# A graph attention kernel: 31 of 512 steps sum both attention products in one accumulator

## The chip, the core and the metric

The kernel runs on one NeuronCore of a Trainium2 chip. TensorE (PE) multiplies, VectorE (DVE) and ScalarE (ACT) work element by element, GpSimd (POOL) does small sums and issues some transfers, and SyncE (SP) issues most of the others. The metric is the device time of one execution in microseconds (us), shorter being better. The kernel before takes 2055.8 us (median of three runs, 2055.79 to 2056.89).

## The reference, cut to what matters

There are 4096 nodes with 512 features, an adjacency matrix A of zeros and ones, and two layers. The change lies in layer 0, an attention with eight heads of 64 features:

```python
feats = jnp.einsum('nf,hfo->hno', X, W)
s_self = jnp.einsum('hno,ho->hn', feats, a_self)
s_neigh = jnp.einsum('hno,ho->hn', feats, a_neigh)
dense = s_self[:, :, None] + s_neigh[:, None, :]
dense = jnp.where(dense > 0, dense, ALPHA * dense)
dense = dense * A[None, :, :]
attn = jax.nn.softmax(dense, axis=-1)
out = jnp.einsum('hij,hjo->hio', attn, feats) + b[:, None, :]
```

After it come a relu, the sum with the input and a layer norm. Layer 1 is an attention among the 128 nodes of each of 32 graphs, with queries, keys and values from 512 x 512 weights, and again a sum and a layer norm.

A pair without an edge has the score 0, so its weight is exp(0) = 1 and not 0. With s the score of the row node, t that of the column node j, E = exp(leaky(s + t)) and f the features of j with the bias, one row of the output is the sum over j of (A (E - 1) + 1) f, divided by the sum of the same weights.

## The kernel before, in words

**What is multiplied.** The kernel writes E as exp(0.2 s) exp(t) max(p, d), where p = exp(0.8 s) depends on the row alone and d = exp(-0.8 t) on the column alone. It divides the whole row by exp(0.2 s); u = exp(-0.2 s) is the factor of what does not carry E. With g = exp(t) f and S the sum of f over all nodes, the numerator is

- `acc`: the sum over j of A max(p, d) g,
- `accf`: minus the sum over j of A f,
- and at the end `y` = (`accf` + S) u + `acc` (lines 1259 and 1267).

**Tiles.** Pairs of heads make four passes (r = 0 to 3), in each of which the 4096 rows come in four chunks of 1024 (c = 0 to 3), and each chunk has 32 steps (j), one for 128 columns of A. A step has a tile `at` of A, 128 x 1024. Its work:

- DVE, line 1475: for each of the two heads one `q` = max(p_row, d) times `at`, 128 x 1024.
- ACT, line 1485 (DVE, line 1480, for the second head of every fourth step): a `mark` that is 1 where A is 1 and p > d, for the sum of the weights.
- PE, line 1499: `accf`, four products of 512 columns, f being held in two parts (`f_s`).
- PE, line 1521: `acc`, eight products of 32 rows of g (`g_s`) with a half of a `q`, four of which stand beside each other in the array.
- PE, line 1536: `dens`, four products of the marks with six numbers of each column, done after every eighth step.

**Stages and cycles.** A setup (to about 156 us) makes features, exponentials and the tables p and u as rows in DRAM (`pu_d`); `p_row` and `u_row` are read back from there for each chunk, spread over all partitions. The first three passes go in cycles of eight steps, the last in groups of four. In a cycle PE does `accf` for all its steps, then `acc` for all, then `dens`. The first pass also turns A: PE transposes (line 610), ACT casts the result to `at` (line 621), and POOL stores it in `at_d`, from which SP loads the tiles of the later passes (line 628). In the second to last chunk of the last pass the groups have pieces of layer 1 between their products, for the two blocks of 512 rows that the chunk before has finished: transposes (line 1075), `zT` (1095 on PE, 1102 on ACT), scores (1122, then `ns` by DVE at 1131 and exponentials by ACT at 1147), values (1167 on PE, `v_t` by DVE at 1175), output (1181 on PE, 1183 on DVE). `PLANS` says which piece stands in which group. After the last chunk a tail of layer 1 alone follows.

**Who waits for whom.** PE executes its instructions as the program is written. The order on DVE, ACT, POOL and SP is made at build time by a planner that goes by priority and by its own costs; each engine then follows its order strictly. `q` has a ring of eight buffers in the first three passes, of six in the last, two being used in each step, so that DVE can be four or three steps ahead of `acc`. `at` has rings of 12 and 6.

**Buffers.** `a4` (line 1080, two of them) holds the diagonal blocks of A for layer 1, `ns` and `pT` (one each) the scores and their transposes. `hst` (one) holds the finished 1024 x 128 tile of a pass. `ck` (two) holds pieces of A that are tested in the passes two to four (line 1222).

Of the kernel before, what the change touches and what calls it, by code (L numbers as in the profile page):

```python
# [404 lines left out]
def adjacency_streamed_path(  # L405
# [55 lines left out]

    g_d = dram.tile([PR, NT // 4, P, 4 * FP], F32, name="g_d")
    f_d = dram.tile([PR, NT // 4, P, 4 * 2 * FP], F32, name="f_d")
    pu_d = dram.tile([2 * H, N], F32, name="pu_d")
    at_d = dram.tile([NCH, NT, P, C], F32, name="at_d")
    hs_d = dram.tile([N, FP * (PR - 1)], F32, name="hs_d")

# [25 lines left out]
    p_all, u_all = pu_all[:, :, 0, :], pu_all[:, :, 1, :]  # L493
    n0 = const.tile([P, NT], F32, name="n0")
    nb_all = const.tile([P, NT, H], F32, name="nb_all")
    e_all = early.tile([P, NT, 2, H], F32, name="e_all")
    e_b = const.tile([P, NT, H, 6], BF16, name="e_b")

# [36 lines left out]
    urowp = ctx.enter_context(tc.tile_pool(name="urows", bufs=1))  # L535
    evp = ctx.enter_context(tc.tile_pool(name="ev", bufs=1))
    hp_ = ctx.enter_context(tc.tile_pool(name="hout", bufs=1))
    ckp = ctx.enter_context(tc.tile_pool(name="ck", bufs=2))
    ps0 = ctx.enter_context(tc.tile_pool(name="ps_misc", bufs=1, space=PSUM))
    banks = [ps0]  # L540

# [90 lines left out]
    with tc.tile_pool(name="setup1", bufs=1, side="right") as one, tc.tile_pool(  # L632
# [97 lines left out]
        def exponentials(k, u, sc):  # L730

            j = 4 * k + u
            if u == 0:
                pu_js[k] = two.tile([P, 4, 2, H], F32, name="pu_j")
            st = small.tile([P, 5, H], F32, name="st")
            for lo, hi, w in ((0, 3, 1), (3, 5, 0)):
                ends_of_setup["DVE", u] = nc.vector.tensor_tensor(
                    st[:, lo:hi].rearrange("p k (q h) -> p k q h", q=2),
                    sc[:, None, :, :, w].to_broadcast([P, hi - lo, 2, H // 2]),
                    powers[:, lo:hi].rearrange("p k (q h) -> p k q h", q=2),  # L740
                    OP.mult,
                )
            nc.scalar.activation(e_all[:, j], st[:, 0:2], AF.Exp)
            nc.scalar.activation(pu_js[k][:, u], st[:, 3:5], AF.Exp)
            nc.scalar.activation(d_all[:, j, :], st[:, 2], AF.Exp)

        def parts_of_exponentials(k):
            blk = slice(4 * k, 4 * k + 4)
            nc.vector.tensor_scalar_mul(
                nb_all[:, blk, :], d_all[:, blk, :], -BIG * (1.0 + 2.0**-23)  # L750
            )
            eb = e_b[:, blk]
            for i in range(2):
                src = e_all[:, blk, i, :]
                rest = small.tile([P, 4, H], F32, name="rest")
                nc.vector.tensor_copy(eb[:, :, :, 3 * i], src)
                nc.vector.tensor_sub(rest, src, eb[:, :, :, 3 * i])
                nc.vector.tensor_copy(eb[:, :, :, 3 * i + 1], rest)
                nc.vector.tensor_sub(eb[:, :, :, 3 * i + 2], rest, eb[:, :, :, 3 * i + 1])
            nc.vector.tensor_copy(  # L760
                e_p[:, blk, :NE].rearrange("p j (m h) -> p j h m", h=H), eb[:, :, :, :3]
            )
            nc.vector.tensor_scalar_mul(eb[:, :, :, :3], eb[:, :, :, :3], -1.0)

        def rows_of_exponentials(k):
            pr = pss.tile([2 * H, 4, P], F32, name="ps_set")
            for u in range(4):
                nc.tensor.transpose(
                    pr[:, u, :], pu_js[k][:, u].rearrange("p k h -> p (k h)"), ident
                )  # L770
            if k < NB - 1:
                row = late.tile([2 * H, 4 * P], F32, name="pu_row")
            else:
                row = hp_.tile([P, CT, FP], F32, name="hst")
                row = row.rearrange("p t n -> p (t n)")[: 2 * H, : 4 * P]
            rows[k] = row
            ends_of_setup["ROW"] = nc.scalar.copy(
                row.rearrange("p (q n k) -> p q k n", q=2, k=2),
                pr.rearrange("p (q k) n -> p q k n", q=2),
            )  # L780
            nc.gpsimd.dma_start(pu_d[:, ts(k, 4 * P)], row)

        def columns_of_exponentials(k, pc=None):
            pc = pss.tile([P, 4, 2 * H], F32, name="ps_set") if pc is None else pc
            for u in range(4):
                nc.tensor.transpose(pc[:, u, :], rows[k][:, ts(u, P)], ident[: 2 * H, : 2 * H])
            nc.vector.tensor_copy(
                pu_all[:, 4 * k : 4 * k + 4].rearrange("p u k h -> p u (k h)"), pc
            )
# [138 lines left out]
    def columns_of_last():  # L928

        columns_of_exponentials(NB - 1, misc([P, 4, 2 * H]))  # L930

    psa = ctx.enter_context(tc.tile_pool(name="ps_acc_f", bufs=1, space=PSUM))
    dens = psa.tile([P, HB], F32, name="dens")
    nc.vector.memset(dens, 0.0)
# [134 lines left out]
    def layer_1(blk, x1b, lp, lp1, lp2):  # L1069
# [45 lines left out]
            if c % 2:  # L1115
                yield
        pq = misc([P, 4, P])
        ns = lp1.tile([P, 4, P], F32, name="ns")
        nm = small.tile([P, 4], F32, name="nm_f")
        for u in range(4):  # L1120
            for f in range(FC):
# [72 lines left out]
        pp = misc([P, 4, P])  # L1194
        for u in range(4):
            nc.tensor.transpose(pp[:, u, :], ns[:, u, :], ident)
        pT = lp1.tile([P, 4, P], F32, name="pT_f")
        nc.scalar.copy(pT, pp)
        values(1)
        yield  # L1200
# [49 lines left out]
    def sums_to_rows(r, c, acc, accf, ae, u_row, later_by):  # L1250
# [25 lines left out]
        def pieces():  # L1276
# [55 lines left out]
            nc.vector.reciprocal(rd, rd)  # L1332
            if r == 0:
                yield later_by
            hst = hp_.tile([P, CT, FP], F32, name="hst")
            for t4 in range(0, CT, 4):
                fin = misc([P, 4, FP])
                for t in range(4):
# [65 lines left out]
    def main_pass(r, ae=None, wide=4):  # L1404

        for c in range(NCH):
# [8 lines left out]
            for h in range(2):  # L1415
                in_order(
                    r == 0 and c < 2,
                    nc.sync.dma_start(
                        u_row[h * FH : (h + 1) * FH, :],
                        broadcast_rows(pu_d[H + 2 * r + h, ts(c, C)], FH, C),  # L1420
                    ),
                )
            def pieces(c, group, place):
                if r == PR - 1 and c:
                    run_plan(PLANS[c == NCH - 1][group][place])
                elif place == (r == 0):
                    run_pieces((0.75 if r else 1.0) * wide)
# [18 lines left out]
            for j0 in range(0, NT, wide):  # L1446
# [13 lines left out]
                    in_order(r == 0 and c == 0 and j0 < 16, ins)  # L1460
                if at_step == 0:
                    cast_steps(0, 6, last_pair)
                follow = [
                    x
                    for x in steps[at_step + wide : at_step + 2 * wide]
# [3 lines left out]
                for j in cycle:  # L1469
                    for h in range(2):  # L1470
                        hh = 2 * r + h
                        q = qs[j, h] = ring("q", qp, 6).tile([P, C], F32, name="q")
                        d_j = d_all[:, j, hh : hh + 1]
                        with following(at_step == 0, ("DVE", 3 if j else 2)):
                            ends_of_setup["Q"] = nc.vector.scalar_tensor_tensor(  # L1475
                                q, p_row[h], d_j, ats[r, c, j].bitcast(F32), op0=OP.max, op1=OP.mult
                            )
                        mark = marks[j, h] = sgp.tile([P, C], FP8, name="mark")
                        if j % 4 == 3 and h == 1:
                            nc.vector.tensor_scalar(  # L1480
                                mark, q, d_j, None, op0=OP.is_gt, saturate=False
                            )
                        else:
                            with following(at_step == 0, "ACT", "ROW"):
                                nc.scalar.activation(  # L1485
                                    mark,
                                    q,
                                    AF.Sigmoid,
                                    bias=nb_all[:, j, hh : hh + 1],
                                    scale=BIG,  # L1490
                                    saturate=False,
                                )
# [1 line left out]
                    with following(True, "Q"):  # L1494
                        parts_of_exponentials(NT // 4 - 1)
                for j in cycle:
                    for w in range(2):
                        for s in range(2):
                            nc.tensor.matmul(  # L1499
                                accf[:, s, :],  # L1500
                                f_s[j // 4][:, j % 4, w, :],
                                ats[r, c, j][:, ts(s, HB)],
                                start=(j == 0 and w == 0),
                                stop=(j == NT - 1 and w == 1),
                            )
# [9 lines left out]
                    pieces(c, j0 // 4, 0)  # L1515

                for j in cycle:
                    for s in range(2):
                        for o in range(0, FP, 32):
                            h = o // FH  # L1520
                            nc.tensor.matmul(  # L1521
                                acc[o : o + 32, s, :],
                                g_s[j // 4][:, j % 4, h, o % FH : o % FH + 32],
                                qs[j, h][:, ts(s, HB)],
                                start=(j == 0),
                                stop=(j == NT - 1),
                            )
                if r == 0:
                    pieces(c, j0 // 4, 1)
# [117 lines left out]
```

## Time and profile before

| | |
|---|---|
| timed runs | 2055.79, 2055.8, 2056.89 us |
| the profiled execution | 2057.91 us, of which 2056.1 us lie between its first and its last instruction |
| PE busy | 2030.4 us (99%) |
| DVE busy | 1671.9 us (81%) |
| ACT busy | 1542.2 us (75%) |
| POOL busy | 224.2 us (11%) |
| granted TensorE clock | 0.994 of full speed |

One execution is recorded; an instruction has a line of the kernel, a start and a length. "Idle before" is the time for which an engine stood still in front of an instruction, and the releaser is what ended it. The chain that ended last is followed back from the last instruction: at each step to what released it, or to the instruction before it on its engine. Instructions of one engine overlap a little at their ends, so that the distance between two starts, and not the length, is what one costs in a dense row.

### The profile page before, as it was taken

Reading aid. Unit: us, or ns where it says so; the run is one execution under the profiler, and the core shown is the slowest. Engines: PE = TensorE matmul, PEld = TensorE weight load, DVE = VectorE, ACT = ScalarE, POOL = GpSimd, SP = SyncE. Lnnn points to the kernel's source line nnn. Section 1 sums busy time; section 2 is a strip of 40 time slices with the busy share of each in tenths; the row PEclk is TensorE's granted clock in tenths of the full one; section 3 lists DMA queues with packets and bytes.
Section 4 is the critical chain, followed back from the end, with each engine's and each line's share of the span. In section 5 each row is a group of like instructions: output and inputs, shape, how many; then the busy total and the mean of one; then the engine's idle time right before and its main releaser. Section 6 shows DMA issues by size and latency. Waiting matters only on the chain.

```text
span 2056.1 us, 38302 instructions
## 1 busy us (share of the span) xinstructions
PE 2030.4 (99%) x15105; PEld 1051.0 (51%) x15105; DVE 1671.9 (81%) x2125; ACT 1542.2 (75%) x1878; POOL 224.2 (11%) x361
## 2 busy tenths in 40 slices
PE   9999999999999999999999999999999999999997
PEld 7884555555544444444454444544454445545453
DVE  5668888888899998798998999999975984896654
ACT  3349888888879889788898989998885666567420
POOL 1222222222100000000000000000210210210111
PEclk9999999999999999999999999999999999999999
DMA  6999999999999999798999999989974764775211
GB/s 208 245 325 259 287 288 276 291 268 289 271 373 337 354 352 335 257 310 298 319 323 340 316 336 323 326 295 358 323 237 144 250 242 137 225 274 169 73 49 43
DMA packets 207371, 551.31 MB, mean 268 GB/s; under 512 B 24780, under 2 KB 65740, under 8 KB 207180
## 3 DMA queue, kind: packets, MB, share of 16 engines
q1 hardware_dynamic: 142828, 426.31, 59.6%
q0 software_dynamic: 62272, 121.91, 23.2%
q8 instruction: 121, 1.98, 0.4%
q10 hardware_dynamic: 2080, 0.52, 0.1%
q14 instruction: 70, 0.57, 0.1%
HBM read 491.79 MB, written 107.22 MB: 291 GB/s over the span
## 4 chain that ended last, share of the span: by engine, by line
PE 93%; DVE 4%; issue 1%; DMA 1%; SPq 0%; POOL 0%; ACT 0%; POOLq 0%; DVEq 0%
PE acc L1521 41%; PE accf L1499 23%; PE ps_fe L800 5%; PE ps_m L1167 5%; PE dens L1536 5%; PE ps_m L1095 5%; DVE q L1475 3%; PE ps_m L1122 1%; PE ps_m L610 1%; PE ps_m L1181 1%; PE ps_m L1075 1%; PE ps_m L1024 1%; PE ps_m L1339 1%; PE ps_set L720 1%; PE ae L1435 1%
## 5 line engine op out<-in xcount | busy, mean ns | idle before, releaser
L1475 DVE SCALAR_TENSOR_TENSOR q<-p_row,d_all,at 128x1024 f32<-128x1024 f32 x1024 | 1242.0, 1277 | 146.9 <-PE acc L1521 121.1
L1485 ACT ACTIVATE mark<-q,nb_all 128x1024 fp8e4<-128x1024 f32 x896 | 995.5, 1145 | 184.3 <-DVE q L1475 168.6
L1521 PE MATMUL acc<-q,g_s 128*32 128x512 f32 x8192 | 903.4, 593 | 1.1 <-DVE q L1475 0.4
L1521 PEld LDWEIGHTS acc<-q,g_s 128*32 128x32 f32 x8192 | 264.1, 110 | 594.4 <-issue 533.0
L1499 PE MATMUL accf<-at,f_s 128*128 128x512 f32 x2048 | 495.2, 398 | 2.1 <-ACT at L621 2.1
L1499 PEld LDWEIGHTS accf<-at,f_s 128*128 128x128 f32 x2048 | 380.3, 188 | 110.4 <-issue 26.4
L1230 ACT ACTIVATE ck<-ck,neg_half_f 128x1024 f32<-128x1024 f32 x128 | 146.0, 1141 | 25.5 <-DMA ck<-in_adj_dram 25.4
L1231 ACT ACTIVATE ck<-ck,neg_quarter 128x1024 f32<-128x1024 f32 x128 | 146.3, 1143 | 1.7
L1536 PE MATMUL dens<-mark,e_b 128*6 128x512 fp8e4 x2048 | 125.3, 379 | 0.0
L800 PE MATMUL ps_fe<-w_sb_f,xT_f 128*128 128x264 f32 (+1 forms) x512 | 121.1, 393 | 1.9 <-ACT xT_f L723 1.9
L621 ACT CAST at<-ps_m 128x1024 fp32r<-128x1024 fp8e4 x124 | 116.4, 1025 | 4.8 <-PE ps_m L610 4.3
L1167 PE MATMUL ps_m<-wvT,x1T 128*128 128x512 f32 x256 | 114.2, 594 | 0.0
L1095 PE MATMUL ps_m<-x1T,M_sb 128*128 128x512 f32 x256 | 112.9, 594 | 0.0
L800 PEld LDWEIGHTS ps_fe<-w_sb_f,xT_f 128*128 128x128 f32 x512 | 100.1, 199 | 16.4 <-ACT xT_f L723 2.5
L1350 POOL DMA_DIRECT2D hs_d<-hst x12 | 10.7, 896 | 847.8 <-DVE hst L1340 847.8
L1480 DVE TENSOR_SCALAR mark<-q,d_all 128x1024 fp8e4<-128x1024 f32 x128 | 96.3, 752 | 4.7
L622 POOL DMA_DIRECT2D at_d<-at x128 | 69.0, 541 | 272.3 <-ACT at L621 248.1
L1536 PEld LDWEIGHTS <-e_b 128*6 128x6 bf16 x2048 | 54.7, 86 | 77.7 <-issue 34.6
L1095 PEld LDWEIGHTS ps_m<-x1T,M_sb 128*128 128x128 f32 x256 | 48.0, 190 | 59.3 <-issue 58.4
L1167 PEld LDWEIGHTS ps_m<-wvT,x1T 128*128 128x128 f32 x256 | 47.6, 190 | 56.4 <-issue 55.2
L1175 DVE TENSOR_TENSOR v_t<-ps_m,bv_row 128x512 f32<-128x512 f32 x32 | 21.7, 684 | 60.5 <-PE ps_m L1167 60.5
L1102 ACT ACTIVATE zT<-ps_m,zb 128x512 f32<-128x512 f32 x32 | 21.7, 680 | 61.2 <-PE ps_m L1095 61.2
(195 smaller groups left out, 1099.5 us busy)
## 6 DMA issues: line engine op xcount, KB each, us to landing
at<-at_d SPq DMA_DIRECT2D x384, 512.0 KB, 6.3
f_s<-f_d SPq DMA_DIRECT2D x128, 512.0 KB, 7.8
at_d<-at POOLq DMA_DIRECT2D x128, 512.0 KB, 14.8
ck<-in_adj_dram SPq DMA_DIRECT2D x128, 512.0 KB, 5.5
g_s<-g_d SPq DMA_DIRECT2D x128, 256.0 KB, 5.6
f_d<-fst POOLq DMA_DIRECT2D x16, 1024.0 KB, 7.9
a_b<-in_adj_dram POOLq DMA_DIRECT2D x32, 512.0 KB, 17.4
p_row<-pu_d SPq DMA_DIRECT2D x32, 512.0 KB, 6.9
```

Of the source, the lines that this page charges most:

```text
L621: ends_of_setup["ACT"] = nc.scalar.copy(at, both[:, :, k])
L800: nc.tensor.matmul(pf[:, q, :, cols], tile_j(xTs[k][:, c].rearrange("p u n -> p (u n)"), u), w_sb[:, c, 4 * q : 4 * q + 4, cols], start=(c ...
L1095: nc.tensor.matmul(pz, L1["M"][:, f, ts(c, P)], x1T[:, f, :], start=(f == 0), stop=(f == FC - 1),)
L1167: nc.tensor.matmul(pv, x1T[:, f, ts(u, P)], L1["wvT"][:, f, :], start=(f == 0), stop=(f == FC - 1),)
L1230: tc.keep_in_program_order(nc.scalar.activation(ck, ck, AF.Square, bias=neg_half))
L1231: nc.scalar.activation(ck, ck, AF.Abs, bias=neg_quarter, accum_out=binp[:, k : k + 1])
L1475: ends_of_setup["Q"] = nc.vector.scalar_tensor_tensor(q, p_row[h], d_j, ats[r, c, j].bitcast(F32), op0=OP.max, op1=OP.mult)
L1480: nc.vector.tensor_scalar(mark, q, d_j, None, op0=OP.is_gt, saturate=False)
L1485: nc.scalar.activation(mark, q, AF.Sigmoid, bias=nb_all[:, j, hh : hh + 1], scale=BIG, saturate=False,)
L1499: nc.tensor.matmul(accf[:, s, :], f_s[j // 4][:, j % 4, w, :], ats[r, c, j][:, ts(s, HB)], start=(j == 0 and w == 0), stop=(j == NT - 1 an ...
L1521: nc.tensor.matmul(acc[o : o + 32, s, :], g_s[j // 4][:, j % 4, h, o % FH : o % FH + 32], qs[j, h][:, ts(s, HB)], start=(j == 0), stop=(j ...
L1536: nc.tensor.matmul(dens[lo : lo + 6, :], e_b[:, j, 2 * r + h, :], marks[j, h][:, ts(s, HB)], start=(j == 0), stop=(j == NT - 1),)
```

## The change

In a folded step `q` is made by two DVE instructions for each head instead of one. With U = 1/u in a new row and 1/exp(t) in a new column, q = (max(p, d) U - 1/exp(t)) A, and q times g is A (E - 1) f. That is the edge's whole share of the numerator, and it belongs to `accf`, which is multiplied by u at the end. So the eight products of line 1521 go into `accf`, and the four of line 1499 are left out. The mark is taken from the sign of q. What the step reads and stores otherwise is as before; `f_s` is loaded for all steps.

Folded are, in the first pass, steps 10 and 18 of the first chunk and 2, 10 and 18 of the others (11), and in the last pass, of the second chunk, one step of group five, two of group six and three of group seven (steps 17; 20, 21; 24 to 26), and of the third and fourth chunk these and step 9 in group three (20 in all).

```diff
+    FOLDED = (0, PR - 1)
+    FOLDS = {4: (1,), 5: (0, 1), 6: (0, 1, 2)}, {2: (1,), 4: (1,), 5: (0, 1), 6: (0, 1, 2)}
+    HU = 2 * len(FOLDED)
...
+            for r in FOLDED:
+                nc.vector.reciprocal(
+                    c_all[r][:, blk], e_all[:, blk, 1, 2 * r : 2 * r + 2]
+                )
...
         def rows_of_exponentials(k):
-            pr = pss.tile([2 * H, 4, P], F32, name="ps_set")
+            for i, r in enumerate(FOLDED):
+                nc.vector.reciprocal(
+                    pu_js[k][:, :, 2 * H + 2 * i : 2 * H + 2 * i + 2],
+                    pu_js[k][:, :, H + 2 * r : H + 2 * r + 2],
+                )
+            pr = pss.tile([2 * H + HU, 4, P], F32, name="ps_set")
...
-        ns = lp1.tile([P, 4, P], F32, name="ns")
+        ns = a4
...
-        pT = lp1.tile([P, 4, P], F32, name="pT_f")
+        pT = a4
...
+            if r == PR - 1:
+                hst = y.rearrange("p (t n) -> p t n", t=CT)
+            else:
+                hst = hp_.tile([P, CT, FP], F32, name="hst")
...
+            def folded(j):
+
+                if r == PR - 1:
+                    return r in FOLDED and c > 0 and j % 4 in FOLDS[c > 1].get(j // 4, ())
+                return r in FOLDED and j % 8 == 2 and (0 if c else 8) < j < NT - 8
+
+            def rows_for_folded():
+
+                for h in range(2):
...
+                    nc.sync.dma_start(
+                        U_row[h],
+                        broadcast_rows(pu_d[2 * H + 2 * FOLDED.index(r) + h, ts(c, C)], P, C),
+                    )
...
+                if any(map(folded, range(NT))) and j0 == (4 if r else 0):
+                    rows_for_folded()
...
+                        if folded(j):
+                            cn = c_all[r][:, j, h : h + 1]
+                            nc.vector.scalar_tensor_tensor(
+                                q, p_row[h], d_j, U_row[h], op0=OP.max, op1=OP.mult
+                            )
+                            nc.vector.scalar_tensor_tensor(
+                                q, q, cn, ats[r, c, j].bitcast(F32), op0=OP.subtract, op1=OP.mult
+                            )
+                            mark = marks[j, h] = sgp.tile([P, C], FP8, name="mark")
+                            nc.scalar.activation(
+                                mark, q, AF.Sigmoid, bias=below_0, scale=2.0**80, saturate=False
+                            )
+                            continue
...
-                    for w in range(2):
+                    for w in range(0 if folded(j) else 2):
...
+                    dst = accf if folded(j) else acc
...
-                                acc[o : o + 32, s, :],
+                                dst[o : o + 32, s, :],
```

The rows U are loaded by SP, two transfers of 512 KB for each chunk that has folded steps: in the first pass into the two buffers of `ck`, which that pass does not use otherwise, and in the last pass into the buffer of `hst` and a new one. For these `ns` and `pT` are given up: they are now written over `a4`, which is therefore held until `pT` has been read. The last pass writes its finished tile over `y`. The pool of `ck` is made after the setup instead of before it.

## The prediction

> **What bounds the kernel now.** I read the page's first two parts and its chain of waits, then the stretches of the four passes, then PE and DVE in order of time in the groups that are to be folded.
>
> ```profile
> PE 2030.4 (99%) x15105; PEld 1051.0 (51%) x15105; DVE 1671.9 (81%) x2125; ACT 1542.2 (75%) x1878; POOL 224.2 (11%) x361
> DVE  5668888888899998798998999999975984896654
> PE 93%; DVE 4%; issue 1%; DMA 1%; SPq 0%; POOL 0%; ACT 0%; POOLq 0%; DVEq 0%
> PE acc L1521 41%; PE accf L1499 23%; PE ps_fe L800 5%; PE ps_m L1167 5%; PE dens L1536 5%; PE ps_m L1095 5%; DVE q L1475 3%; PE ps_m L1122 1%; PE ps_m L610 1%; PE ps_m L1181 1%; PE ps_m L1075 1%; PE ps_m L1024 1%; PE ps_m L1339 1%; PE ps_set L720 1%; PE ae L1435 1%
> L1475 DVE SCALAR_TENSOR_TENSOR q<-p_row,d_all,at 128x1024 f32<-128x1024 f32 x1024 | 1242.0, 1277 | 146.9 <-PE acc L1521 121.1
> ```
>
> PE is the chain from end to end, and 23% of the chain is `accf`, which the change cuts. DVE's main row waits 121.1 us for PE (for a free `q`), so it is ahead of PE. Whether it stays ahead is a question for each stage (window, then busy time of PE, PEld, DVE, ACT, POOL, clock, DMA share, GB/s): a chunk of the first pass, and one of the last.
>
> ```profile
> 266.00:372.00 106.00, 105.66 (x977) 53.49 (x976) 88.08 (x92) 92.48 (x91) 25.75 (x41) 1.00 1.11 280
> 1605.00:1775.00 170.00, 169.65 (x1028) 83.42 (x1028) 127.55 (x197) 109.55 (x148) 22.28 (x37) 1.00 0.63 215
> ```
>
> PE is full in both; DVE has some 18 us of 106 free in the first, 42 of 170 in the second.
>
> In order of time, the first cycle of a chunk of the first pass, PE then DVE:
>
> ```profile
> 371.06 7.60 PE L1499 MATMUL accf<-at,f_s 128*128 128x512 f32 x32
> 378.50 1.07 PE L610 MATMUL ps_m<-ident_b,a_b 128*128 128x128 bf16 x16
> 379.49 13.94 PE L1521 MATMUL acc<-q,g_s 128*32 128x512 f32 x128
> ...
> 370.67 6.06 DVE L1475 SCALAR_TENSOR_TENSOR q<-p_row,d_all,at 128x1024 f32<-128x1024 f32 x5
> 376.83 0.90 DVE L1480 TENSOR_SCALAR mark<-q,d_all 128x1024 fp8e4<-128x1024 f32 x1
> 381.52 10.85 DVE L1475 SCALAR_TENSOR_TENSOR q<-p_row,d_all,at 128x1024 f32<-128x1024 f32 x9 [3.80 <-PE acc L1521]
> ```
>
> DVE fills its eight buffers, stands for 3.80 us, and goes on when the first step of `acc` frees two. In the last pass (DVE, then PE, third chunk, group six):
>
> ```profile
> 1694.06 3.68 DVE L1475 SCALAR_TENSOR_TENSOR q<-p_row,d_all,at 128x1024 f32<-128x1024 f32 x3 [3.68 <-issue]
> 1698.32 6.06 DVE L1475 SCALAR_TENSOR_TENSOR q<-p_row,d_all,at 128x1024 f32<-128x1024 f32 x5
> 1708.29 0.29 DVE L1131 CUSTOM_DVE_ANT_0 ns<-ps_m,a 128x128 f32<-128x128 f32 x1 [3.91 <-PE ps_m L1122]
> ...
> 1699.90 3.91 PE L1499 MATMUL accf<-at,f_s 128*128 128x512 f32 x16
> 1708.18 7.07 PE L1521 MATMUL acc<-q,g_s 128*32 128x512 f32 x64
> ```
>
> **What the Trainium skill says.** "VectorE: DVE Perf Modes", section "The perf-mode tier table", gives two-tensor fp32 instructions one element per cycle and no faster mode. The trace agrees: 128x1024 takes 1277 ns, and nine stand in 10.85 us, a pitch of (10.85 - 1.28) / 8 = 1.197 us. Its section "The DRAIN you can't avoid" says that an instruction starts only when the pipe of the one before is empty. Here that holds for dependent ones alone: line 512 after 1183, whose result it reads, starts 0.78 us behind a start of 0.75 us length, while independent q's overlap by 0.08. So the second of a folded pair costs 1.2 us when the planner puts something between and about 1.3 if not. "TensorE: Matmul & The Clock Gate", "Part 3: Packing small matmuls", lets products in different column groups run at once; 128 of line 1521 in 13.87 us are 0.434 us for each four, and a change of the target bank alters nothing in that. "DMA: Bandwidth & Descriptors", "Issuing engines are not separate DMA queues": all transfers share the 16 engines. In the first pass these show a share of 1.11, so the added 1 MB per chunk, beside 280 GB/s x 106 us = 30 MB, is not free of risk.
>
> **The change part by part.** *Removed on PE:* four `accf` products a step. In the first pass 32 take 378.50 - 371.06 = 7.44 us from start to start, 0.93 a step; in the last 16 take 1664.26 - 1660.53 = 3.73 (group four of that chunk), also 0.93. 31 x 0.93 = 28.8 us. The products into `accf` cost what they cost in `acc`.
>
> *Added on DVE:* two instructions a step, 2 x 1.2 to 1.3 = 2.4 to 2.6 us; ACT makes as many marks as before.
>
> *First pass (11 steps).* The folded step is the third of its cycle, so it falls into the filling of the buffers, where DVE then stands 3.80 (above), 4.86 and 5.19 us. Of 3.80, 2.4 to 2.6 go to the added pair and 0.93 to PE's earlier `acc`: 0.3 to 0.5 are left. Behind that lies another half: step eight of `acc` is due at 379.49 + 7 x 1.734 = 391.6, and its q's end at 391.1. I take no loss. If that cover were gone, each us is paid in full.
>
> *Last pass, group five:* DVE has 3.7 to 7.6 us free (3.68 in the fence), 2.4 to 2.6 are used. Nothing is lost.
>
> *Group six (two folds, 4.8 to 5.2 us):* DVE has eight q's to make from 1694.06 on and ends at 1704.3; folded, at 1709.1 to 1709.5. PE needs 9.13 us from the end of `acc` at 1699.05 to the next, now 7.27: 1706.3. Steps one to three are ready in time, the third by 0.5. Then line 1131 holds DVE for 0.95, and the fourth step's q's (2.4) end at 1712.5 to 1712.9, due at 1706.3 + 3 x 1.75 = 1711.6. PE waits 0.9 to 1.3, unless the planner puts the q's first: I take 0.95, three times, 2.85 us. Late next are `ns` and its exponentials, by about 1.5 us; they are used by line 1196 some 20 us later.
>
> *Group seven (three folds, 7.2 to 7.8 us):* DVE stands 10.41 us in front of `v_t` in the second and third chunk and 9.88 in the fourth. Hidden.
>
> *Group three (one fold, third and fourth chunk):* DVE's six q's end at 1647.24 and both `v_t` follow; folded, the q's end at 1649.7 and `v_t` at 1650.4, while PE wants it for line 1181 at 1650.86 - 0.93 = 1649.9. PE waits about 0.55, twice: 1.1 us.
>
> *Setup:* 32 tiny reciprocals, 0.6 us of each 17 us block in which DVE is busy for two thirds; hidden but for the last block. There the ROW copy of line 777 starts at 156.23 right behind a cast that ended then, and the two reciprocals (0.18 us for four elements, line 1160) stand before its transposes: I take 0.5 us on the chain to the first `accf`.
>
> *SP and buffers:* 14 transfers U_row. In the first pass they come when step 18 of the chunk before frees `ck`, 40 us ahead of use; for the first chunk behind the bias row of 167.24, used at about 187, with 7 us to land. In the last pass they come a chunk ahead. Behind them in SP's queue stand `f_s`, `g_s` and `at` loads; `f_s` is issued near 402 and used at 424.6, so some us of standing are covered. Holding `a4` until `pT` is read moves the loads of line 1080 (1538.79, 1595.45 and so on) to about 1596, 1652 and, for the last block, from 1947 to 1967, where the next loads behind it (1969.09) are not issued earlier anyway. Writing over `y` needs only what was transposed. These cost nothing; the cover is the queue's own waiting.
>
> Sum: 28.8 - 2.85 - 1.1 - 0.5 = 24.35 us. The profiled span goes from 2056.1 to 2031.8; its run took 2057.91, and the median of the runs, 2055.8, goes to **2031.5**.
>
> **The rivals.** *All hidden:* the planner puts `v_t` and the q's that PE waits for first. Then 28.3, 2027.5. For it: each stall above is under 1.3 us. Against: it plans by its own costs, and already now PE waits for q's (2.4 us at 1467, 1.4 at 1614).
>
> *The first pass gives nothing:* the margin of 0.3 us is eaten, by a late U_row, by the loaded DMA engines, or because ACT's marks come later and its casts (line 621) behind them keep PE's transposes waiting. Then 28.8 - 10.2 - 4.45 = 14.1: 2041.7. Against it: 4.86 and 5.19 us in the other cycles, and ACT's 13 us of 106 free.
>
> *The last pass gives its saving back:* DVE's order there is perturbed and the stalls are 18.6 instead of 3.95 us. Only the first pass counts, 9.7: 2046.
>
> *Slower:* in the last pass the longer q's come to stand in front of rows that PE waits for (1131, 1175, 520). Place: groups three and five to seven. The price is the added DVE time that shows, of 20 x 2.6 = 52 us; from 55% of it on (28.3 us) the kernel loses. At 65%: 2061. Against it: DVE's 10.41 us in front of `v_t`, which hold the largest part.
>
> *The change doesn't do what it says:* all folded steps leave `accf`'s products out in the written order of PE, so this rival is only a term of the above.
>
> **How the numbers follow.** The forecast has 0.50 (2028.5 to 2034.5), all hidden 0.18, the first pass giving nothing 0.13, the last giving its saving back, wholly or in part, 0.12, slower 0.06; 0.01 is left for no change. A measurement tells about 0.2% (4 us) from none, and all cases but the last two are beyond it: faster 0.93, same 0.01, slower 0.06. The range runs from 2027 (all hidden) to 2042 (first pass giving nothing, and half of the last pass's case).
>
> **What would show it.** Line 1499 should have 2048 - 124 = 1924 products and 29 us less; line 1521 the same 8192. DVE should be busy some 75 us longer and its idle time before q should fall by about as much as it is covered. In the first pass a chunk should take 103.4 instead of 106.2 us, with DVE still standing before the first q of `acc`, a few tenths in the first cycle. In groups three and six PE should wait 0.5 to 1.3 us for `v_t` and q. I am wrong if PE shows gaps of over 1 us in group five or seven, if U_row ends waits of DVE, or if the tail after the last `dens` (1933.5 to the end) becomes longer than its 122.6 us.

## The result and the profile after

The changed kernel takes 2042.7 us (median of six runs, 2038.29 to 2044.16), the kernel before 2055.8 us (six runs, 2053.32 to 2057.68): a ratio of 0.993, 95% interval 0.992 to 0.995. It is faster by 13 us, where 24 were forecast. The profiled execution took 2043.19 us, its span 2041.3 us, 14.8 us less than before.

The page's busy times, DVE in slices and the chain of waits, of the changed kernel:

```profile
PE 2005.9 (98%) x14981; PEld 1030.0 (50%) x14981; DVE 1744.8 (85%) x2219; ACT 1533.1 (75%) x1872; POOL 231.0 (11%) x362
...
DVE  5668898898999998798999989999997897889754
...
PE 85%; DMA 7%; DVE 5%; issue 1%; ACT 1%; SPq 0%; POOL 0%; POOLq 0%; DVEq 0%; ACTq 0%
...
L1534 DVE SCALAR_TENSOR_TENSOR q<-p_row,d_all,at 128x1024 f32<-128x1024 f32 x962 | 1168.1, 1279 | 106.0 <-PE acc L1581 78.8
...
L1558 PE MATMUL accf<-at,f_s 128*128 128x512 f32 x1924 | 469.3, 400 | 1.7 <-ACT at L628 1.6
```

DVE has 73 us more to do and still waits 78.8 us for PE. `accf` has its 1924 products. New are the transfers, 7% of the chain instead of 1%. Where they stand is told by PE's waits from 150 to 600 us (waited for, us in all, times, longest); the first row and the third are new:

```profile
PE ps_m L617 <- DMA a_b<-in_adj_dram: 6.2, 3, 3.6
PE accf L1558 <- ACT at L628: 1.6, 1, 1.6
PE ps_set L786 <- DVE pu_j L780: 1.2, 1, 1.2
PE ps_m L617 <- DVE hst L1312: 1.1, 3, 0.4
```

PE waits for the pieces of A that are to be turned (`a_b`, loaded by POOL at line 605), once in the first cycle of each chunk but the first. The worst of the three, in order of time on PE, where the prediction showed 371.06 to 379.49 of the kernel before:

```profile
369.24 7.01 PE L1558 MATMUL accf<-at,f_s 128*128 128x512 f32 x28
379.89 1.07 PE L617 MATMUL ps_m<-ident_b,a_b 128*128 128x128 bf16 x16 [3.63 <-DMA a_b<-in_adj_dram]
380.88 5.31 PE L1581 MATMUL acc<-q,g_s 128*32 128x512 f32 x32
386.02 1.89 PE L1581 MATMUL accf<-q,g_s 128*32 128x512 f32 x16
```

The saving is in the first line, 28 products in place of 32. Behind it PE stands for 3.63 us, and the next 32 products take 5.31 us, where the same 32 in the fourth chunk take 3.64.

The stretches, each from the first `accf` product of one pass to that of the next (us):

| | before | after | forecast gain | gain |
|---|---|---|---|---|
| setup, to the first product | 157.8 | 160.2 | -0.5 | -2.4 |
| first pass | 424.0 | 422.8 | 10.2 | 1.2 |
| second and third pass | 772.3 | 772.5 | 0 | -0.2 |
| last pass and tail | 702.0 | 685.8 | 14.65 | 16.2 |
| span | 2056.1 | 2041.3 | 24.35 | 14.8 |

So the last pass gave somewhat more than forecast, the setup lost 2 us more, and nine of the first pass's ten microseconds are missing. By chunk the first pass took 107.1, 106.2, 106.3 and 104.4 us before and takes 104.7, 104.4, 109.3 and 104.4 now: the third chunk loses 3 us, where each should gain 2 to 3.

### The profile page after: what moved, and what is told of

The parts are those of the page before. It is cut to its first block, busy times and chain, and to the rows that moved or that the text cites. A ratio compares the mean times of both kernels' runs of the same rounds, so it can differ in the third digit from the quotient of the medians.

```text
span 2041.3 us, 38200 instructions
## 1 busy us (share of the span) xinstructions
PE 2005.9 (98%) x14981; PEld 1030.0 (50%) x14981; DVE 1744.8 (85%) x2219; ACT 1533.1 (75%) x1872; POOL 231.0 (11%) x362
## 4 chain that ended last, share of the span: by engine, by line
PE 85%; DMA 7%; DVE 5%; issue 1%; ACT 1%; SPq 0%; POOL 0%; POOLq 0%; DVEq 0%; ACTq 0%
PE acc L1581 35%; PE accf L1558 20%; PE ps_fe L818 5%; PE ps_m L1186 5%; PE ps_m L1114 5%; PE dens L1597 5%; DMA a_b<-in_adj_dram 4%; DVE q L1534 3%; PE accf L1581 2%; PE ps_m L1141 1%; PE ps_m L1200 1%; DMA hp_l<-hs_d 1%; PE ps_m L617 1%; DMA at_d<-at 1%; PE ps_m L1043 1%
## 5 line engine op out<-in xcount | busy, mean ns | idle before, releaser
L1534 DVE SCALAR_TENSOR_TENSOR q<-p_row,d_all,at 128x1024 f32<-128x1024 f32 x962 | 1168.1, 1279 | 106.0 <-PE acc L1581 78.8
L1544 ACT ACTIVATE mark<-q,nb_all 128x1024 fp8e4<-128x1024 f32 x834 | 926.8, 1144 | 174.7 <-DVE q L1534 160.1
L1581 PE MATMUL acc<-q,g_s 128*32 128x512 f32 x7696 | 853.7, 594 | 1.1 <-DVE q L1534 0.4
L1581 PEld LDWEIGHTS acc<-q,g_s 128*32 128x32 f32 x7696 | 250.2, 110 | 557.2 <-issue 496.3
L1558 PE MATMUL accf<-at,f_s 128*128 128x512 f32 x1924 | 469.3, 400 | 1.7 <-ACT at L628 1.6
L1558 PEld LDWEIGHTS accf<-at,f_s 128*128 128x128 f32 x1924 | 357.2, 189 | 107.3 <-issue 27.8
L818 PEld LDWEIGHTS ps_fe<-w_sb_f,xT_f 128*128 128x128 f32 x512 | 100.5, 200 | 16.2 <-ACT xT_f L730 2.3
L1529 ACT ACTIVATE mark<-q,below 128x1024 fp8e4<-128x1024 f32 x62 | 69.6, 1153 | 24.5 <-DVE q L1525 24.2
L1525 DVE SCALAR_TENSOR_TENSOR q<-q,c_all,at 128x1024 f32<-128x1024 f32 x62 | 77.3, 1273 | 0.0
```

The source lines that it names most:

```text
L818: nc.tensor.matmul(pf[:, q, :, cols], tile_j(xTs[k][:, c].rearrange("p u n -> p (u n)"), u), w_sb[:, c, 4 * q : 4 * q + 4, cols], start=(c ...
L1534: ends_of_setup["Q"] = nc.vector.scalar_tensor_tensor(q, p_row[h], d_j, ats[r, c, j].bitcast(F32), op0=OP.max, op1=OP.mult)
L1544: nc.scalar.activation(mark, q, AF.Sigmoid, bias=nb_all[:, j, hh : hh + 1], scale=BIG, saturate=False,)
L1558: nc.tensor.matmul(accf[:, s, :], f_s[j // 4][:, j % 4, w, :], ats[r, c, j][:, ts(s, HB)], start=(j == 0 and w == 0), stop=(j == NT - 1 an ...
L1581: nc.tensor.matmul(dst[o : o + 32, s, :], g_s[j // 4][:, j % 4, h, o % FH : o % FH + 32], qs[j, h][:, ts(s, HB)], start=(j == 0), stop=(j ...
```

## Experiments

Each time is the median of its runs, with the lowest and the highest; the ratio is that to the kernel before, run beside it, with its 95% interval. Stretches and waits are those of the one profiled execution.

Three explanations for the missing nine. D1: the transfers were full before, and whatever PE saves it waits. D2: the 1 MB of U rows that the change adds to each chunk makes `a_b` late. D3: the folded steps' marks, which come later on ScalarE, delay the casts behind them, the stores that POOL issues, and so the `a_b` loads in POOL's queue.

### Only the last pass folded, and three cuts in the first pass

The base of the next kernels:

```diff
-    FOLDED = (0, PR - 1)
+    FOLDED = (PR - 1,)
```

> Only the 20 steps of the last pass are folded; the first pass, its reciprocals and its U rows are as before. All theories: the first pass of the changed kernel gained only 0.5 us, the last pass and the tail 16.3 us, so this kernel takes what the changed one takes, 2042 us (2040 to 2044). If instead the first pass's folded steps were worth their 10.2 us in the time and the loss is elsewhere, 2052 us.

2042.49 us (2041.87 to 2045.47), ratio 0.9945 (0.9929 to 0.9962). The 11 folded steps of the first pass are worth nothing. This kernel is the yardstick for the first pass: 423.0 us, no wait for `a_b`.

The changed kernel with the U rows of the first chunk used in all four:

```diff
+                if r == 0 and c:
+                    U_row.extend(rows_of_chunk_0)
+                    return
```

> The changed kernel with the U rows of the first pass loaded for its first chunk only and used again in the other three (which leaves out what those chunks should be multiplied with). DMA engines full already before (D1): 3 MB less of some 160 MB, so at most 3 us of gain and the waits for the tiles a_b stay: 2041 to 2043. The 1 MB of each chunk is what delays the a_b loads (D2): the waits for a_b vanish, 2034 us (2032 to 2036). Folded marks on ScalarE delay the casts, the stores and so the loads (D3): nothing changes, 2042.7.

2033.92 us (2033.15 to 2036.29), ratio 0.9898 (0.9881 to 0.9914). No wait for `a_b` is left and the first pass takes 414.7 us. That is what D2 said, and D1 is out.

The base with PE's part alone, the four `accf` products of the 11 steps left out:

```diff
-                    for w in range(0 if folded(j) else 2):
+                    for w in range(0 if folded(j) or left_out(j) else 2):
```

> As the kernel with the last pass folded alone, and in the first pass the four accf products of the same 11 steps are left out (their share of minus the sum of A f is missing from the result); VectorE, ScalarE and all transfers are as before. TensorE has 10.2 us less work and nothing else changes. D1, DMA full: PE waits for a_b instead, the same time as the last pass alone within 2 us, 2041 to 2043. D2 and D3: the whole 10.2 us appear, 2032 us (2031 to 2034).

2034.53 us (2032.83 to 2035.51), ratio 0.9899 (0.9883 to 0.9916); first pass 415.1 us, 8.0 less than the base. The transfers had room for a shorter PE. Both this run and the one before reach 8.0 to 8.4 of 10 us; in the first cycle of a chunk some 0.6 of the 0.9 is kept, and why was not looked into.

The changed kernel with every second f tile of the first pass not loaded:

```diff
+                    if r == 0 and k % 2 and (c or k > 3):
+                        f_s[k] = f_s[k - 1]
```

> The changed kernel with every second tile of f in the first pass not loaded (its steps use the tile before, so the result of the first pass is wrong): 2 MB of transfers less in each chunk, all else the same. D1 and D2, transfers set the pace: the a_b waits shrink or vanish, 2034 us (2032 to 2038). D3, ScalarE's order sets it: nothing changes, 2041.5 to 2043.5.

2029.81 us (2027.47 to 2030.22), ratio 0.9876 (0.9859 to 0.9892), faster than its range. Other bytes than the U rows serve as well: no wait for `a_b`, first pass 414.0 us. The rest of its lead over the kernel with the rows loaded once lies outside the first pass: its profiled setup ended at 157.5 instead of 160.6, with a granted clock of 1.00 between 20 and 45 us, where that one and the changed kernel show 0.86, and its last pass took 684.0 instead of 686.7 us. Whether the edit has a part in that is open.

### The rows without the shorter PE

If the rows alone make `a_b` late, they must do so while PE has all its work. Two attempts failed. The first loads the rows and uses them nowhere:

```diff
-                return r in FOLDED and j % 8 == 2 and (0 if c else 8) < j < NT - 8
+                return False
...
-                if any(map(folded, range(NT))) and j0 == (4 if r else 0):
+                if (r == 0 or any(map(folded, range(NT)))) and j0 == (4 if r else 0):
```

> The kernel with the last pass folded alone, to which the U rows of the first pass are loaded as in the changed kernel, but nothing reads them. C, a budget: with the rows, the transfers of a chunk need some 105.5 us (the changed kernel's chunk), which still fits into the 105.8 to 106.3 us that TensorE needs when no step is folded: no wait for a_b, the time of the kernel without the rows, 2042.5 us (2041 to 2044). B, a burst: 1 MB issued at once makes the next a_b loads late at any pace: waits for a_b of some us in chunks two to four, 2046 to 2050 us.

2057.52 us (2054.01 to 2060.15), ratio 1.0010 (1.0001 to 1.0019), which nobody expected. With no reader to wait for, SP issued the rows of all four chunks between 169.9 and 193.9 us; PE's waits for the whole execution begin with

```profile
PE accf L1558 <- DMA f_s<-f_d: 12.2, 1, 12.2
```

that is, the f tile of the second cycle stood behind the rows in SP's queue. Chunks two to four, now without any rows to load, took 106.2, 106.3 and 104.4 us as in the base. The second attempt gives the rows a reader, a copy of two numbers where the folded steps would be:

```diff
+                        if touched(j):
+                            nc.vector.tensor_copy(small.tile([P, 2], F32, name="nm_f"), U_row[h][:, :2])
```

> As the kernel with U rows that nothing reads, but two numbers of each row are read by VectorE where the folded steps of the changed kernel would be, so that the rows of a chunk are loaded when those of the chunk before have been used, as in the changed kernel. C, a budget: with the rows the transfers of a chunk need some 105.5 us, less than the 105.8 to 106.3 us of an unfolded chunk on TensorE: 2042.5 us (2041 to 2044), no wait for a_b beyond 1 us. B, a burst makes the loads behind it late at any pace: a_b waits of 2 us or more in a chunk, 2047 to 2050 us.

2065.09 us (2063.59 to 2065.82), ratio 1.0051 (1.0034 to 1.0067). The planner put all these copies, which depend on nothing but the rows, into the first chunk, and DVE waited there six times, 32.7 us in all, for transfers that came behind others. Both kernels say nothing on the question, but they show what a misplaced megabyte costs.

The third keeps everything of the change except PE's saving:

```diff
-                    for w in range(0 if folded(j) else 2):
+                    for w in range(0 if folded(j) and r else 2):
...
-                    dst = accf if folded(j) else acc
+                    dst = accf if folded(j) and r else acc
```

> The changed kernel with VectorE's, ScalarE's and the transfers' part of the first-pass folding left as it is, but TensorE does the four accf products of the 11 steps all the same and sums their q into acc (so A f is counted in excess there). C, a budget: 105.5 us of transfers fit behind 105.8 to 106.3 us of TensorE, no wait for a_b: the time of the kernel with the last pass folded alone, 2042.5 us (2041 to 2044), and TensorE waits only where its work is shortened and the rows are loaded as well. B, the rows as such, or the folded marks on ScalarE, make the a_b loads late: the 6.2 us of a_b waits stay on top of the full work, 2048 to 2051 us.

2042.17 us (2040.45 to 2043.48), ratio 0.9934 (0.9918 to 0.9951): the base's time, first pass 423.1 us, no wait for `a_b`, though the rows were loaded chunk by chunk (from 170.6, 216.7, 321.4 and 427.7 us). B is out: the rows and the folded steps' work on DVE and ScalarE, without the shorter PE, cost nothing. But it was close. PE, and POOL's issue of the load in question, in the third chunk of this kernel:

```profile
373.55 7.60 PE L1558 MATMUL accf<-at,f_s 128*128 128x512 f32 x32
380.99 1.07 PE L617 MATMUL ps_m<-ident_b,a_b 128*128 128x128 bf16 x16
...
353.29 0.90 POOL L605 DMA_DIRECT2D a_b<-in_adj_dram  x1 [0.64 <-DMA at_d<-at]
354.29 0.55 POOL L629 DMA_DIRECT2D at_d<-at  x1
362.52 0.53 POOL L629 DMA_DIRECT2D at_d<-at  x1 [7.69 <-DMA a_b<-in_adj_dram]
```

The load landed 27.6 us after its issue, at 380.9; PE turned its tile at 380.99. The last line shows the other half of the mechanism: POOL issues in order, and a store that has to wait for an earlier load holds up what stands behind it. The same load in five kernels (issue and landing from POOL's transfers, the time PE turns the tile, or would without waiting, from PE in order of time):

| third chunk | issued | us to landing | landed | PE wants it | margin |
|---|---|---|---|---|---|
| before | 350.2 | 13.9 | 364.1 | 378.5 | 14.4 |
| short PE alone | 348.5 | 16.8 | 365.3 | 376.2 | 10.9 |
| changed, rows once | 348.5 | 24.1 | 372.6 | 376.3 | 3.6 |
| changed, PE not shortened | 353.3 | 27.6 | 380.9 | 381.0 | 0.1 |
| changed | 352.9 | 26.9 | 379.8 | 376.3 | -3.5 |

(The last 376.3 is 379.89 - 3.63.) The margin of 14.4 us is eaten by three parts, taken in this order of kernels: 3.5 by the shorter PE, 7.3 by what folding changes on DVE, ScalarE and in POOL's rhythm, 7.1 by the rows. With the rows taken back, or PE's saving, PE does not wait; folding taken back with the rows kept was not run. That is D2, with D3 as an accomplice and not, as I had set it, an alternative. Why folding without rows lengthens the landing from 16.8 to 24.1 us was not taken apart; POOL's stores there wait for marks and for earlier `a_b` loads as in the changed kernel. The rows of the first chunk, which that kernel still loads, are hardly the reason: where, without folding, the rows of all chunks came in the first one, the third chunk's load took 13.7 us.

The rows do not delay this load by being under way beside it. In the changed kernel those of the third chunk were issued at 318.0 and 319.3 us and had landed by 328.1, 25 us before the load was issued. The delay is handed on, and the starts and landings of POOL's transfers show by what. In every kernel here each POOL transfer starts only after the one eight places before it has landed, by 0.5 us or more, so that at most eight are under way: the store at 362.52 above is the eighth behind the load of 340.8 us, which landed at 362.0. From 160 to 580 us 27% of POOL's issues find seven others under way in the kernel before, 42% with the short PE alone, 70% with the rows loaded once, 80% with PE not shortened and 83% in the changed kernel. While seven others are under way, a transfer that lands later puts off the next issue, whatever made it late. The row for it among POOL's waits of the changed kernel from 150 to 600 us (the kernel before has none such):

```profile
POOL at_d L629 <- DMA a_b<-in_adj_dram: 72.2, 10, 9.9
```

Whether the limit of eight is set by the chip or by the program, these runs do not show.

### The setup, group three, and the third pass

U by an exponential of ScalarE instead of DVE's reciprocals, on the base:

```diff
-                nc.vector.reciprocal(
-                    pu_js[k][:, :, 2 * H + 2 * i : 2 * H + 2 * i + 2],
-                    pu_js[k][:, :, H + 2 * r : H + 2 * r + 2],
-                )
+            nc.scalar.activation(pu_js[k][:, u, 2 * H :], st[:, 4], AF.Exp, scale=-1.0)
```

> The kernel with the last pass folded alone, with the U columns made by ScalarE (an exponential more for each 128 nodes) instead of VectorE's reciprocals ahead of TensorE's transposes. If these reciprocals are what TensorE waits for in the setup (2.3 us in two waits), 2040 us (2039 to 2041.5) and no wait for pu_j by VectorE; if the setup is late for another reason, 2042.5.

2040.52 us (2039.56 to 2042.98), ratio 0.9932 (0.9916 to 0.9949); the waits for `pu_j` are gone and the first product starts at 156.3 instead of 160.2. The intervals of this kernel and of the base overlap, and the first product of the four kernels with this setup starts at 154.8 to 158.3, of those with the reciprocals at 157.5 to 161.1; the vanished waits, 2.3 us, are the firmer evidence. They are not all gain, though: the granted clock between 20 and 45 us is 0.93 here and 0.86 in the base, worth 25 x 0.07 = 1.7 us of the 3.9, and in the first pass PE waits 1.6 us for `pu_all`, as before the change (1.7), which the base does not; the first pass takes 424.0 instead of 423.0 us. In the changed kernel the two waits were these, on PE in order of time:

```profile
43.77 0.60 PE L786 MATMUL ps_set<-ident_f,pu_j 128*20 128x128 f32 x4 [1.22 <-DVE pu_j L780]
...
157.94 0.60 PE L786 MATMUL ps_set<-ident_f,pu_j 128*20 128x128 f32 x4 [1.22 <-DVE pu_j L780]
```

Group three not folded, on the base:

```diff
-    FOLDS = {...}, {2: (1,), 4: (1,), 5: (0, 1), 6: (0, 1, 2)}
+    FOLDS = {...}, {4: (1,), 5: (0, 1), 6: (0, 1, 2)}
```

> The kernel with the last pass folded alone, without step 9 (group three) in its last two chunks. K, the saving of group three is kept but for 0.3 us in each: 2 x (0.93 - 0.3) = 1.3 us more, 2043.8, and the wait of dens for the mark by VectorE at the end of group four stays. L, it is given back at that wait, since the x1b additions on VectorE come when hp_l has landed and not earlier: the waits shrink to below 0.5 us and the time stays, 2042.5.

2042.76 us (2039.58 to 2045.54), ratio 0.9938 (0.9919 to 0.9957): by the time alone nothing can be told. In the profile the group takes 13.7 and 13.8 us in the two chunks, in the base 13.2 and 13.1, and the group behind it 20.4 to 20.5 in both kernels. So K: group three keeps 0.5 to 0.7 of its 0.93. The wait of `dens` for DVE's mark that both theories spoke of, 2.5 us in the changed kernel, is absent from the base itself, so this run could not undo it.

Steps 11 and 19 of each chunk of the third pass folded too, U by ScalarE:

```diff
-    FOLDED = (PR - 1,)
+    FOLDED = (2, PR - 1)
+    MIDDLE = (11, 19)
```

> As the kernel with the U columns by ScalarE, and two steps (11 and 19) in each chunk of the third pass folded too: 8 x 0.93 = 7.4 us less on TensorE; in these steps VectorE's own mark goes to ScalarE, so VectorE adds 2 x (2.4 - 0.75) = 3.3 us to a chunk in which it is idle 6.5 us of 93.9, and the transfers of that pass are 16 MB of at and not 33 MB of a_b and at_d. All kept: 2032.6 us (2031 to 2034). VectorE has no time to spare where it counts: waits for q eat it, 2040. The U rows delay the loads of at as they do those of a_b: waits for at, 2036 to 2040.

2034.98 us (2034.28 to 2037.24), ratio 0.9905 (0.9889 to 0.9922). No wait for `at`; but the third pass goes from 375.6 to 371.7 us, half of what was expected. The cycle with step 19 takes 22.2 instead of 23.1 us, the one with step 11 24.4 instead of 24.5: there DVE also makes the chunk before into rows, and had 1.1 us to spare instead of the 2.4 of the next cycle.

### A kernel that pays for its rows

U by ScalarE; the first pass folded, with two of its eight f tiles kept in memory over the four chunks, which takes away as many bytes as the rows add; steps 19 and 27 of the third pass folded.

```diff
+    HELD = (2, 3)
+    MIDDLE = (19, 27)
...
+                    if r == 0 and k in HELD and c:
+                        f_s[k] = held[k]
```

> All that the runs so far point to: U columns by ScalarE; the first pass folded as in the changed kernel, but with two of the eight f tiles held in memory over its four chunks (1 MB less of transfers in chunks two to four, as much as the U rows add); the third pass with steps 19 and 27 folded; the last pass as in the changed kernel. C: no a_b waits, the first pass gains 8.4 us as with the rows loaded once, the third pass 4 x 1.8 = 7.2 us: 2040.5 - 15.6 = 2025 us (2023 to 2027). If it is not the number of bytes that makes the a_b loads late but the two rows arriving together, the first pass gains nothing and it takes 2033 us.

2027.94 us (2022.84 to 2031.37), ratio 0.9866 (0.9846 to 0.9887): faster than both kernels, 3 us above what was expected. The third pass gains its 7.1 us (368.5), the first only 4.5 (419.5 against 424.0 with U by ScalarE alone): in the third chunk one wait for `a_b` was left. The load came 26.7 us after its issue at 349.6, and the margin is -2.2 us, only 1.3 better than in the changed kernel, though the chunk moves no more bytes than before the change. PE there:

```profile
376.39 1.83 PE L619 MATMUL ps_m<-ident_b,a_b 128*128 128x128 bf16 x16 [2.24 <-DMA a_b<-in_adj_dram]
378.15 4.48 PE L1596 MATMUL acc<-q,g_s 128*32 128x512 f32 x32
```

With a g tile held as well and less of two f tiles loaded, 0.5 MB less in a chunk than before the change:

```diff
+                    if r == 0 and k == HELD[0] and c:
+                        g_s[k] = held["g", k]
...
+                        for us in (slice(0, 2), slice(3, 4)) if r == 0 and folded(4 * k + 2) else (slice(0, 4),):
```

> As the kernel in which the U rows are paid for, with one g tile held as well and the f tiles of the folded steps loaded without them, where not held: 0.5 MB less in a chunk than before the change. C, the pace of the transfers was just short in one chunk: the remaining a_b wait of 2.2 us, and the 4 us that it cost in the third chunk, go: 2024 us (2022 to 2026), with less spread. If the bytes do not decide, 2028 as before.

2027.51 us (2025.4 to 2028.13), ratio 0.9862 (0.9846 to 0.9879). The wait is gone (the load lands at 370.6, a margin of 4.0 us) and the first pass takes 415.5 us, 4.0 less, as expected; but the time is that of the kernel above within its spread, and the profiled span only 1.8 us shorter. The first chunk of the last pass, in which nothing is folded, takes 98.7 us here, 97.1 in the kernel above and 95.1 in the one with U by ScalarE alone. On DVE in order of time, a row addition stands in front of q's and waits for its transfer:

```profile
1383.77 0.56 DVE L1266 SCALAR_TENSOR_TENSOR x1b<-hp_l,x1b 128x384 f32<-128x384 f32 x1 [3.26 <-DMA hp_l<-hs_d]
1384.25 3.67 DVE L1559 SCALAR_TENSOR_TENSOR q<-p_row,d_all,at 128x1024 f32<-128x1024 f32 x3
```

The planner set a different order there. Without these 3.6 us this kernel would be near the 2024 expected; that is an estimate and was not run.

## Where the prediction was right and where it was wrong

The direction was right, the size was not: the time came out at 2042.7 us, 0.7 above the upper end of the range and 11 above the forecast of 2031.5. It lies beside the rival "the first pass gives nothing" (2041.7), to which I had given 0.13.

**PE's saving** was right: 1924 products, 0.91 to 0.93 us from each folded step where nothing waits (25.8 to 24.9 us for such a cycle). The page has 25.9 us less for the row (495.2 to 469.3), where I wrote 29; lengths overlap and are modelled, and the distance between starts is what counts.

**First pass: the step that failed** is "these cost nothing; the cover is the queue's own waiting". I asked when the U rows land, and they did land in time: no DVE wait names them. I did not ask whose transfers they delay. I had read the DMA share of 1.11 as "not free of risk" and worked out no margin. The share could not have told it: between 372 and 478 us it is 1.11 or 1.12 in the changed kernel, in the one with the rows loaded once, with a short PE alone and with PE not shortened, and only the first waits. The margin could have been had from the trace: the `a_b` load of the third chunk landed 14.4 us before its use. The rows took 7.1 of it, the folding itself 7.3 and the shorter PE 3.5. As a term of the sum: 10.2 us were forecast, 0.2 came against the base (423.0 to 422.8). What I had cited of the Trainium skill, "DMA: Bandwidth & Descriptors", section "Issuing engines are not separate DMA queues", was the right thing to look at: SP's loads made POOL's late, by 2.8 us from issue to landing and 4.4 us in the issue itself (349 to 353 us, 24.1 to 26.9), the delay being handed on in POOL's queue. I put the rival's weight on DVE's margins of 4.86 and 5.19 us, which were good, as the run with the rows loaded once shows.

**Last pass:** forecast 14.65, measured 16.2. Group six did not wait the 0.95 us, since the planner put the q's ahead of the scores' rows, the exception that I had named. Group three kept 0.5 to 0.7 of 0.93, forecast 0.38. Groups five and seven showed nothing, as said. Not foreseen: at the end of group four `dens` waits in each of the three folded chunks for DVE's mark, because a row addition stands ahead of it and its operand, saved rows of the passes before, has not landed. PE's and DVE's waits after 1355 us of the changed kernel (us in all, times, longest), and then DVE in order of time in its fourth chunk:

```profile
PE dens L1597 <- DVE mark L1539: 2.5, 3, 1.5
...
DVE x1b L1265 <- DMA hp_l<-hs_d: 14.3, 7, 3.7
```

```profile
1834.66 0.56 DVE L1265 SCALAR_TENSOR_TENSOR x1b<-hp_l,x1b 128x384 f32<-128x384 f32 x1 [3.70 <-DMA hp_l<-hs_d]
1835.13 0.75 DVE L1539 TENSOR_SCALAR mark<-q,d_all 128x1024 fp8e4<-128x1024 f32 x1
```

These waits are 2.5 us here and absent from the base, whose last pass gained 17.7 (702.0 to 684.3). Against that, 1.7 us came in the first chunk of this pass (96.8 to 95.1), which has no folded step, in two groups of which the trace names no wait; that stays open. The tail was 121.5 us, not longer.

**Setup:** 0.5 forecast, two waits of 1.22 us found. I reckoned with one pair of reciprocals in the last block; the first block, at 43.77, has no cover either. In the first cycle behind the setup two more differences nearly cancel: a 1.7 us wait for `pu_all` is gone, and the first 32 products take 10.20 instead of 9.18 us, at a lower clock.

## What to carry to other kernels

Before adding a transfer, find the transfers with the least time between landing and use in that stage, and reckon with their margin, not with that of the new one alone; the mean DMA share does not show it. A margin shared by several edits hides them: here the shorter PE alone, the shorter PE with the folding, and the folding with the rows made PE wait for no `a_b`, and all three together did. Where a new transfer is worth it, take bytes away elsewhere in the same stage (as many as the rows add removed two of the three waits, half a megabyte more the third), and see that it is issued when it is needed: a megabyte for each chunk, issued four at once, cost 15 us. Where an engine's transfers wait for earlier ones of its own, count how often its queue is full.

## What the runs showed of the hardware

A wait of PE can cost more than its length. In these profiles the granted clock is either full or half, and all its changes within one profile lie whole multiples of 3.41 us apart. Cut at such instants (window, then busy time of PE, PEld, DVE, ACT, POOL, clock, DMA share, GB/s), the changed kernel around its waits of 3.63 us in the third chunk and 2.19 us in the fourth, and then the kernel that pays for its rows around its wait of 2.24 us:

```profile
377.47:380.88 3.41, 0.99 (x16) 0.90 (x16) 0.70 (x1) 1.38 (x3) 0.51 (x1) 1.00 1.09 343
380.88:384.29 3.41, 3.41 (x18) 0.79 (x20) 0.00 (x0) 3.15 (x4) 0.67 (x3) 0.50 1.03 417
...
483.27:486.68 3.41, 2.32 (x11) 1.46 (x9) 3.38 (x3) 3.41 (x5) 0.00 (x0) 1.00 1.14 262
486.68:490.09 3.41, 2.31 (x29) 1.31 (x32) 0.75 (x1) 2.83 (x4) 1.04 (x2) 1.00 1.04 415
...
373.07:376.48 3.41, 1.17 (x7) 0.65 (x7) 2.88 (x3) 3.39 (x4) 0.00 (x0) 1.00 1.09 341
376.48:379.90 3.42, 3.42 (x28) 1.92 (x32) 0.00 (x0) 2.45 (x3) 1.08 (x2) 0.50 1.03 422
```

3.41 us at half the clock lose 1.7 us, just what the 32 products took more (5.31 against 3.64). With it the three waits account for 6.2 + 1.7 = 7.9 of the 8.1 us by which the first pass of the changed kernel stands above that with the rows loaded once (422.8 and 414.7). The Trainium skill, "TensorE: Matmul & The Clock Gate", section "HAM oscillation — how this bites in real kernels", gives gaps of over some 3.4 us as what lowers the clock. The 3.63 us agree, and the 2.19 us in the fourth chunk, after which the clock stayed at 1.00; but the 2.24 us of the kernel that pays for its rows were followed by the same 3.41 us at half. So the measurement says that shorter gaps can cost it too. What sets the last two apart in the lines is their place: the 2.24 us lie within one stretch, in which PE worked 1.17 of 3.41 us, while the 2.19 us are shared by two, with 2.3 us of work in each. Three waits make no threshold: a stretch with only 1.4 us of work, from 1968.1 us of the changed kernel on, was followed by the full clock.
